# Layer 0's experts by slots and one-expert tiles instead of all experts for all tokens

## Chip, core and metric

The kernel runs on one core of one Trainium2 chip. The metric is the device time of one execution in microseconds. The engines have the profile's names: PE is TensorE (PEld its weight loads), DVE VectorE, ACT ScalarE, POOL GpSimd, SP SyncE; a name with q (SPq, POOLq) is that engine's queue, where DMAs are issued.

## What is computed

Four images of 256 channels and 32 x 32 pixels pass through two layers. Layer 0 is attention in which each row keeps its largest scores, and then a mixture of 8 experts on the 4096 tokens. Layer 1 is a selective scan in four directions, and then a second mixture of 8 experts. Everything is float32. The part that the change concerns is layer 0's mixture:

```python
def _moe(tokens, router_w, w1, b1, w2, b2):      # tokens 4096 x 256, 8 experts
    logits = tokens @ router_w.T
    probs = softmax(logits)
    rw, re = top_k(probs, 2)
    rw = rw / maximum(rw.sum(-1), 1e-12)
    combine = zeros.at[token, re].set(rw)         # two weights per token, six zeros
    out = tokens
    for e in range(8):
        h = gelu(tokens @ w1[e] + b1[e])          # 256 -> 256
        y = h @ w2[e] + b2[e]                     # 256 -> 256
        out = out + combine[:, e:e + 1] * y
    return out

t = t + _moe(_ln_t(t), ...)                       # _ln_t: layer norm over the channels
```

So each token needs two of the eight experts; the other six are multiplied by zero. Layer 1's mixture has the same form, with 1024 hidden channels.

## The kernel before

The program is one long straight line of five stages. The images stay in SBUF as `x[b]`, channels on the partitions (two groups of 128), 1024 tokens along the row. A tile framework allocates buffers from pools (`bufs` is the number of buffers of one name), puts in semaphores, and orders the instructions of each engine by its own priorities, except inside `manual_schedule`, where the written order holds.

**Attention (0 to 1912.6 us)** has a hand-written order. Near its start (`i == 3`, L882) SP issues one DMA that fills `slots_x`, a buffer of 33 MB in DRAM, with zeros from SBUF; layer 1 needs it later. The four residual loads `x_res` (L422) follow on SP's queue over the stage. At the end a value `bad` is loaded into a register of every engine, and a branch (L1066) skips a slow alternative.

**Layer 0's experts (1912.6 to 2522.5 us)** are dense. For each image `layer_norm` writes the normalised tokens `tn[b]`, and matmuls (L1217) give the logits of all images in one PSUM tile. `top2` makes from them `comb`, the two weights of each token and zeros elsewhere. `start_acc` sets the accumulator to the sum of the weighted second biases. Then the loops run over 8 experts, 4 images and 2 halves of 512 tokens:

- L1241: four matmuls `hp` (128 x 128 weights, 512 tokens), as two output groups by two input groups
- L1243: `Gelu` on ACT into `hid`
- L1248: eight matmuls `y`, two for each 128 tokens, now with the tokens on the partitions
- L1250: DVE adds `y` times the token's weight to `acc`

A float32 matmul appears as two records in the profile. Weights of an expert (512 KB) are loaded two experts ahead. In the last expert's loop `acc` is transposed back and added to `x[b]` (L1258, L1260). After image 0, `Prep(0)` prepares the first scan: a layer norm over channels, projections and softplus (`delta`, `dx`).

**Scans (2522.5 to 3782 us)** have a hand-written order as well. DVE's scans set it. While image b + 1 is scanned, `norm(b)` and `route(b)` of layer 1 run step by step in between (each `yield` is one step): `norm` makes the layer norm and the logits of an image, with the tokens as rows of 258 numbers in `tok`; `route` finds the two best experts of each token and gives each (token, choice) pair a *slot*, a row of `slots_x`. Each expert has a region of 16 blocks of 256 slots. `scatter` writes each token's row to its two slots, one indirect DMA on POOL for 128 rows.

**Layer 1's experts (3782 to 4329 us)** then work on tiles of T = 256 slots of one expert. A table, filled by `Tiles.fill`, says for tile i which expert and which block it takes; SP loads the two numbers into registers and issues the DMAs with them as addresses. At most 39 tiles (`NTILE`) are possible; 36 (`USUAL`) always run, and the others behind a branch on `extra`. Tiles whose blocks are full early start before the last image is routed. The results go by indirect DMAs to two rows per token in `results` (L1751).

**The final read (4329 to 4373 us)** loads `results` in eight pieces of 1 MB with four buffers (L1804), weights and adds the two rows of each token (L1808, L1809), transposes them (L1812), adds to `x[b]` (L1815) and writes the output (L1816). Reads and writes are both issued by SP, in turn.

Of the kernel before, what the change touches and what calls it, by code (L numbers as in the profile page):

```python
# [21 lines left out]
P = 128  # L22
# [36 lines left out]
def metaformer(ctx: ExitStack, tc: tile.TileContext, t: dict, out: bass.AP):  # L59
# [70 lines left out]
    def top2(lg, pool):  # L130

        def t3(name):
            return pool.tile([P, NTA, E], F32, tag=name, name=name)

        def t2(name):
            return pool.tile([P, NTA], F32, tag=name, name=name)

        def wide(a):
            return a.unsqueeze(2).to_broadcast([P, NTA, E])

        prob, red = t3("tk_prob"), t2("tk_red")
        nc.vector.tensor_reduce(red, lg, AX.X, ALU.max)
        nc.vector.tensor_tensor(prob, lg, wide(red), ALU.subtract)
        nc.scalar.activation(prob, prob, AF.Exp)
        nc.vector.tensor_reduce(red, prob, AX.X, ALU.add)
        nc.vector.reciprocal(red, red)
        nc.vector.tensor_tensor(prob, prob, wide(red), ALU.mult)

        score, rest, comb = t3("tk_score"), t3("tk_rest"), t3("tk_comb")
        order = first.unsqueeze(1).to_broadcast([P, NTA, E])  # L150

        def best(src, value, onehot):

            nc.vector.tensor_reduce(value, src, AX.X, ALU.max)
            nc.vector.tensor_tensor(score, src, wide(value), ALU.is_equal)
            nc.vector.tensor_tensor(score, score, order, ALU.mult)
            nc.vector.tensor_reduce(red, score, AX.X, ALU.max)
            nc.vector.tensor_tensor(onehot, score, wide(red), ALU.is_equal)

        m1, m2, hot1, hot2 = t2("tk_m1"), t2("tk_m2"), t3("tk_hot1"), t3("tk_hot2")  # L160
        best(prob, m1, hot1)
        nc.vector.scalar_tensor_tensor(rest, hot1, -2.0, prob, ALU.mult, ALU.add)
        best(rest, m2, hot2)
        tot = t2("tk_tot")
        nc.vector.tensor_tensor(tot, m1, m2, ALU.add)
        nc.vector.tensor_scalar(tot, tot, 1e-12, None, ALU.max)
        nc.vector.reciprocal(tot, tot)
        nc.vector.tensor_tensor(comb, hot1, hot2, ALU.add)
        nc.vector.tensor_tensor(comb, comb, prob, ALU.mult)
        nc.vector.tensor_tensor(comb, comb, wide(tot), ALU.mult)  # L170
        return comb


    def start_acc(acc, comb, b2, pool, psum, tag):
        for g in range(NTA // 4):
            ct_ps = psum.tile([E, 4, P], F32, tag=tag, name="ct_ps")
            for i in range(4):
                nc.tensor.transpose(ct_ps[:, i, :], comb[:, g * 4 + i, :], ident)
            ct = pool.tile([E, 4, P], F32, tag="ct", name="ct")
            nc.scalar.copy(ct, ct_ps)  # L180
            for i in range(4):
                y0 = psum.tile([P, C], F32, tag=tag, name="y0")
                nc.tensor.matmul(y0, ct[:, i, :], b2, start=True, stop=True)
                nc.scalar.copy(acc[:, g * 4 + i, :], y0)

    dram = ctx.enter_context(tc.tile_pool(name="slots", bufs=1, space=bass.MemoryType.DRAM))
    slots_x = dram.tile([(E * BLOCKS + 1) * T, W], F32, tag="slots_x", name="slots_x")
    results = dram.tile([2 * B * L + 2 * P, C], F32, tag="results", name="results")  # L190
# [10 lines left out]
    with ExitStack() as st:  # L201
# [644 lines left out]
        with tc.manual_schedule():  # L846
# [33 lines left out]
            for i in range(len(order) + 8):  # L880
                if i == 3:
                    nc.sync.dma_start(slots_x.rearrange("(a p) c -> p a c", p=P),  # L882
                                      zeros.unsqueeze(1).to_broadcast([P, (E * BLOCKS + 1) * T // P, W]))
                turn(i)
# [185 lines left out]
    rt = ctx.enter_context(tc.tile_pool(name="rt", bufs=1))  # L1070
    of_scans = ExitStack()
# [117 lines left out]

    with ExitStack() as st:  # L1190
        wp = st.enter_context(tc.tile_pool(name="m0_w", bufs=1))
        p2 = st.enter_context(tc.tile_pool(name="m0_p2", bufs=2))
        psl = st.enter_context(tc.tile_pool(name="m0_psl", bufs=1, space=PSUM))
        ps2 = st.enter_context(tc.tile_pool(name="m0_ps2", bufs=2, space=PSUM))
        ps3 = st.enter_context(tc.tile_pool(name="m0_ps3", bufs=3, space=PSUM))

        rw = load_rows(wp, "rw0", E)
        b1 = load(wp, "b1_0", [P, E, CT])
        b2 = load(wp, "b2_0", [E, C])

        def weights(e):
            w1 = p2.tile([P, CT, C], F32, tag="w1", name="w1", bufs=3)
            w2 = p2.tile([P, CT, C], F32, tag="w2", name="w2", bufs=3)
            nc.sync.dma_start(w1, t["w1_0"][e].rearrange("(c p) f -> p c f", p=P))
            nc.sync.dma_start(w2, t["w2_0"][e].rearrange("(c p) f -> p c f", p=P))
            return w1, w2

        ahead = [weights(0), weights(1)]

        tn = [wp.tile([P, CT, L], F32, tag=f"tn{b}", name=f"tn{b}") for b in range(B)]  # L1210
        lg = psl.tile([P, NTA, E], F32, tag="lg", name="lg")
        for b in range(B):
            layer_norm(tn[b], x[b], 1e-5, p2, ps2, "m")
            nc.gpsimd.tensor_tensor(x[b], x[b], tn[b], ALU.add)
            for n in range(NT):
                for c in range(CT):
                    nc.tensor.matmul(lg[:, b * NT + n, :], tn[b][:, c, ts(n, P)], rw[:, c, :],  # L1217
                                     start=(c == 0), stop=(c == CT - 1))
        comb = top2(lg, wp)
        acc = wp.tile([P, NTA, C], F32, tag="acc", name="acc")  # L1220
        start_acc(acc, comb, b2, p2, ps2, "m")
        preps = [Prep(0)]

        def room(name, shape):

            if name == "ln_sq":
                return tn[0]
            return p2.tile([P, *shape], F32, tag="ln_sq" if name == "xm" else name, name=name,
                           bufs=1 if name == "sp" else None)

        for e in range(E):
            w1, w2 = ahead.pop(0)
            if e + 2 < E:
                ahead.append(weights(e + 2))
            for b in range(B):
                for h in range(NHALF):
                    hid = p2.tile([P, CT, HALF], F32, tag="hid", name="hid", bufs=3)
                    for f in range(CT):
                        hp = ps3.tile([P, HALF], F32, tag="hp", name="hp")
                        for c in range(CT):  # L1240
                            nc.tensor.matmul(hp, w1[:, c, ts(f, P)], tn[b][:, c, ts(h, HALF)],  # L1241
                                             start=(c == 0), stop=(c == CT - 1))
                        nc.scalar.activation(hid[:, f, :], hp, AF.Gelu, bias=b1[:, e, f : f + 1])  # L1243
                    for i in range(4):
                        n = b * NT + h * 4 + i
                        y = ps2.tile([P, C], F32, tag="y", name="y")
                        for f in range(CT):
                            nc.tensor.matmul(y, hid[:, f, ts(i, P)], w2[:, f, :],  # L1248
                                             start=(f == 0), stop=(f == CT - 1))
                        nc.vector.scalar_tensor_tensor(acc[:, n, :], y, comb[:, n, e : e + 1], acc[:, n, :],  # L1250
                                                       ALU.mult, ALU.add)
                if e < E - 1:
                    continue
                for c in range(CT):
                    for h in range(NHALF):
                        tp = ps2.tile([P, 4, P], F32, tag="m", name="tp")
                        for i in range(4):
                            nc.tensor.transpose(tp[:, i, :], acc[:, b * NT + h * 4 + i, ts(c, P)], ident)  # L1258
                        xs = x[b][:, c, ts(h, HALF)]
                        nc.vector.tensor_tensor(xs, tp.rearrange("p a b -> p (a b)"), xs, ALU.add)  # L1260
                if b == 0:
                    for _ in preps[0].steps(room, ps2, "m"):
                        pass

    rw1 = load(cons, "rw1", [P, CT, E], t["wr1"].rearrange("(c p) o -> p c o", p=P))
    brs = load(cons, "brs", [P, E], t["br1"][0].partition_broadcast(P))

    def kept(name, shape, dt=F32):
        return rt.tile([P, *shape], dt, tag=name, name=name)

    tok = kept("tok", [NT, W])
# [616 lines left out]
```

## Time and profile before

Three runs took 4373.1 us in the median (4371.8 to 4384.0); the profiled execution spans 4373.0 us. Its busy times by stage, from the table of stretches:

| stage | us | PE busy | DVE busy | ACT busy | POOL busy | PE clock | GB/s |
|---|---|---|---|---|---|---|---|
| attention | 1912.6 | 1511.7 | 1592.1 | 1650.7 | 885.1 | 0.79 | 24 |
| layer 0's experts | 609.9 | 588.5 | 185.7 | 168.0 | 18.9 | 0.93 | 8 |
| scans | 1259.5 | 1213.3 | 1152.8 | 914.0 | 624.0 | 0.99 | 112 |
| layer 1's experts | 547.0 | 532.1 | 80.8 | 152.0 | 84.4 | 1.00 | 187 |
| final read | 44.0 | 15.5 | 23.4 | 13.6 | 0 | 0.50 | 286 |

A row is read as a stage with its own limit: an engine that is busy for nearly all of it can set its length, and one that is busy for little cannot. Matmuls are pipelined, so the busy time of a group over its count is the time that one takes from TensorE, while the mean in nanoseconds is its latency. The clock is the share of full speed that was granted to TensorE.

### The profile page before, as it was taken

The page shows a single profiled execution, that of the slowest core. Times are in us where ns is not written, and L with a number is a line of the kernel's source. Part 1 is how long each engine was busy: PE and PEld are TensorE (multiplying, and loading weights), DVE is VectorE, ACT ScalarE, POOL GpSimd, SP SyncE. Part 2 cuts the span into 40 slices and gives each one's busy share as a digit, 9 for nine tenths or more (in the row PEclk, how much of TensorE's full clock was granted, in tenths as well). Part 3 has the DMA queues.
Part 4 walks back from the last instruction along what each step waited for, and adds up shares of the span by engine and source line. Part 5 has one row for each costly group of instructions (what it writes and reads, how often), then busy time and mean ns, then how long its engine had stood idle before and what let it go on. Part 6 is the DMA issues. An engine that isn't in the chain of part 4 may idle for free. (4 is left out here: it accounts for less than half of the span.)

```text
span 4373.0 us, 51176 instructions
## 1 busy us (share of the span) xinstructions
PE 3861.1 (88%) x18522; PEld 2148.5 (49%) x18522; DVE 3034.8 (69%) x5121; ACT 2898.3 (66%) x3800; POOL 1612.4 (37%) x1257
## 2 busy tenths in 40 slices
PE   8378878888888788688999989999999999999996
PEld 5143434343434344345666534444444443588885
DVE  2788898889988988922222489989989989611112
ACT  2989998999999989722111567776877776432222
POOL 0246454644554455520000034444544545321110
PEclk9578877887788778886999999999999999999997
DMA  9200000000000000000000033333423333555555
GB/s 290 72 1 1 11 1 1 1 10 1 1 1 11 1 1 1 11 19 1 10 10 5 2 103 105 119 103 113 128 97 115 121 112 116 178 185 184 192 188 185
DMA packets 171769, 306.80 MB, mean 70 GB/s; under 512 B 27753, under 2 KB 116594, under 8 KB 171506
## 3 DMA queue, kind: packets, MB, share of 16 engines
q1 hardware_dynamic: 161184, 284.10, 20.9%
q0 software_dynamic: 6528, 17.90, 1.1%
q8 instruction: 149, 2.44, 0.2%
q10 hardware_dynamic: 3794, 1.42, 0.1%
q14 instruction: 114, 0.93, 0.1%
HBM read 246.68 MB, written 56.69 MB: 69 GB/s over the span
## 5 line engine op out<-in xcount | busy, mean ns | idle before, releaser
L542 POOL TENSOR_SCALAR dr<-s_n,last 128x1024 bf16<-128x1024 f32 x256 | 731.1, 2873 | 865.1 <-DVE state L570 398.4
L458 ACT ACTIVATE junk_a<-s_n,state 128x1024 int8<-128x1024 f32 x448 | 514.7, 1149 | 27.6 <-DVE state L570 8.0
L1552 POOL TENSOR_TENSOR uu<-dx,bb 128x1024 f32<-128x1024 f32 x128 | 302.4, 2363 | 528.4 <-ACT a_log L1499 528.4
L1585 POOL TENSOR_TENSOR da_c<-prod,come 128x1024 f32<-128x1024 f32 x128 | 244.3, 1909 | 487.6 <-DVE h L1591 433.1
L462 DVE TENSOR_SCALAR_CACHE_REDUCE junk_v<-s_n,state 128x1024 int8<-128x1024 f32 x320 | 408.7, 1277 | 8.8
L1740 ACT ACTIVATE hid<-hp,b 128x256 f32<-128x256 f32 x288 | 133.5, 473 | 355.9 <-PE hp L1738 355.3
L509 DVE SCALAR_TENSOR_TENSOR w<-s_n,win 128x1024 f32<-128x1024 f32 x256 | 352.1, 1375 | 5.3
L1250 DVE SCALAR_TENSOR_TENSOR acc<-y,tk_comb,acc 128x256 f32<-128x256 f32 x256 | 121.0, 484 | 335.9 <-PE y L1248 332.0
L512 DVE MAX8 win<-w 128x8 f32<-128x1024 f32 x256 | 314.5, 1228 | 8.8
L610 ACT ACTIVATE ex<-sT 128x1024 f32<-128x1024 f32 x256 | 246.9, 1015 | 91.5 <-PE sT L602 91.5
L458 ACT ACTIVATE junk_a<-s_n,guess 128x1024 int8<-128x1024 f32 x256 | 294.2, 1149 | 7.4
L1243 ACT ACTIVATE hid<-hp,b 128x512 f32<-128x512 f32 x128 | 87.7, 687 | 318.8 <-PE hp L1241 318.4
L1565 DVE TENSOR_TENSOR_SCAN h<-da,uu 128x1024 f32<-128x1024 f32 x128 | 290.6, 2271 | 4.2 <-DMA cb<-bc_d 4.2
L1591 DVE TENSOR_TENSOR_SCAN h<-da_c,uu 128x1024 f32<-128x1024 f32 x128 | 291.0, 2274 | 0.0
L1574 DVE TENSOR_TENSOR_SCAN h<-da,uu 128x1024 f32<-128x1024 f32 x128 | 289.8, 2264 | 0.0
L620 PE MATMUL o_ps<-ex,vT 128*32 128x256 f32 x2048 | 238.4, 447 | 47.6 <-ACT ex L610 38.1
L1248 PE MATMUL y<-w,hid 128*128 128x256 f32 x1024 | 267.0, 397 | 3.5 <-ACT hid L1243 2.5
L1539 ACT ACTIVATE da_c<-delta,a_log 128x1024 f32<-128x1024 f32 x128 | 268.1, 2095 | 2.5 <-DVE a_log L1500 2.4
L1595 PE MATMUL hp<-h,ident 128*128 128x512 f32 x512 | 248.5, 608 | 22.5 <-DVE h L1591 22.3
L1738 PE MATMUL hp<-xe,w 128*128 128x256 f32 x1152 | 258.6, 381 | 6.4 <-DVE xe L1726 6.2
L492 ACT COPY s_n<-sp 128x1024 f32<-128x1024 f32 x256 | 245.4, 1003 | 24.7 <-PE sp L484 13.2
L1560 PE MATMUL hp<-h,twice 128*128 128x512 f32 x512 | 243.9, 599 | 18.3 <-DVE h L1565 18.2
(519 smaller groups left out, 7946.2 us busy)
## 6 DMA issues: line engine op xcount, KB each, us to landing
bb<-bc_d SPq DMA_DIRECT2D x128, 512.0 KB, 5.0
cb<-bc_d SPq DMA_DIRECT2D x128, 512.0 KB, 4.2
w<-in_w SPq DMA_DIRECT2D x36, 1024.0 KB, 5.3
w2e<-in_w SPq DMA_DIRECT2D x36, 1024.0 KB, 5.6
slots_x<-zeros SPq DMA_DIRECT2D x1, 33282.0 KB
y<-results SPq DMA_DIRECT2D x8, 1024.0 KB, 8.0
xs<-slots_x SPq DMA_DIRECT2D x19, 258.0 KB, 5.4
b2e<-in_b SPq DMA_DIRECT2D x36, 128.0 KB, 5.3
```

What stands on the lines that cost most here:

```text
L458: nc.scalar.activation(junk, self.row(r), AF.Sign, bias=thr, scale=-1.0, accum_out=u)
L462: nc.vector.tensor_scalar(junk, self.row(r), thr, None, ALU.is_lt, ALU.add, accum_out=u)
L509: nc.vector.scalar_tensor_tensor(w, self.row(r), self.win[:, r, 0:1], self.row(r), ALU.is_gt if r < LAST_DVE else ALU.is_ge, ALU.subtract, ...
L512: nc.vector.max(out=self.win[:, r, 1:], in_=w)
L542: ins = nc.gpsimd.tensor_scalar(dr, self.row(r), self.last[:, r : r + 1], None, ALU.is_lt)
L1248: nc.tensor.matmul(y, hid[:, f, ts(i, P)], w2[:, f, :], start=(f == 0), stop=(f == CT - 1))
L1539: nc.scalar.activation(grid(self.da_c), cols_flipped(self.prep.delta[:, self.c]), AF.Exp, scale=self.decay)
L1552: nc.gpsimd.tensor_tensor(self.uu[:, 0], self.prep.dx[:, self.c], self.bb, ALU.mult)
L1565: nc.vector.tensor_tensor_scan(rows.rearrange("p r w -> p (r w)"), self.da, self.uu[:, 0], 0.0, ALU.mult, ALU.add)
L1574: nc.vector.tensor_tensor_scan(hs[:, ::-1], self.da[:, ::-1], self.uu[:, 0][:, ::-1], 0.0, ALU.mult, ALU.add)
L1591: nc.vector.tensor_tensor_scan(hs, self.da_c, self.uu[:, 1], 0.0, ALU.mult, ALU.add)
L1738: nc.tensor.matmul(hp[:, f % 2], self.w1[:, c, ts(f, P)], self.xe[:, c], start=(c == 0), stop=(c == CT - 1))
```

## The change

Layer 0 is given layer 1's method. The definitions of `norm`, `route` and `Tiles` move ahead of layer 0 and get a parameter for the layer; `top2` and `start_acc` go. For each image the tokens are normalised and routed, and a critical section on POOL scatters its rows into `slots_x0` by 16 indirect DMAs and waits for their landing. After the fourth image a table `every` of 39 entries is filled, and the tiles run: SP loads block and expert into registers, reads 256 slots and the expert's weights, and writes the tile's result to the same block of `slots_y0`. The biases of all experts stay in SBUF; DVE, which loads the expert's number as well, copies the two that a tile needs. At the end 64 indirect reads fetch each token's two results, and DVE weights and adds them. Both DRAM buffers are filled with zeros during attention, so that unused slots hold numbers. Separately, the final read gets eight buffers and issues all its loads at once, and the output DMAs move to POOL's queue.

```diff
             for i in range(len(order) + 8):
+                if i in (20, 36):
+                    nc.sync.dma_start((slots_x0 if i == 20 else slots_y0).rearrange("(a p) c -> p a c", p=P),
+                                      zeros[:, :C].unsqueeze(1).to_broadcast([P, (E * BLOCKS + 1) * T // P, C]))
...
-        for b in range(B):
-            layer_norm(tn[b], x[b], 1e-5, p2, ps2, "m")
-            nc.gpsimd.tensor_tensor(x[b], x[b], tn[b], ALU.add)
-            for n in range(NT):
...
-        comb = top2(lg, wp)
-        acc = wp.tile([P, NTA, C], F32, tag="acc", name="acc")
-        start_acc(acc, comb, b2, p2, ps2, "m")
...
+        for b in range(B):
+            d = pb.tile([P, CT, L], F32, tag="d", name="d")
+            here = slot0[:, :, ts(b, NT)]
+            for _ in norm(b, 0, tokens[b], pb, ps_n, "t", "t", d):
+                pass
+            for _ in route(b, 0, None, here, wp.tile([P, 1536], F32, tag="numbers", name="numbers"), ps_n, "t"):
+                pass
+
+            with tc.tile_critical(name=f"scatter{b}", no_gpsimd_drain=True):
+                for n in range(NT):
+                    for k in range(2):
+                        nc.gpsimd.indirect_dma_start(
+                            out=slots_x0, out_offset=bass.IndirectOffsetOnAxis(ap=here[:, k, n : n + 1], axis=0),
+                            in_=tokens[b][:, n], in_offset=None).then_inc(scattered, 16)
+                nc.gpsimd.wait_ge(scattered, 16 * 2 * NT * (b + 1))
...
+        def tile0(i):
...
+            block = register(1, E * BLOCKS, [mybir.EngineType.SP])
+            xs = pb.tile([P, T // P, C], F32, tag="xs", name="xs", bufs=4)
+            nc.sync.dma_start(xs, blocks_x[bass.ds(block, 1)].rearrange("o p a c -> p (o a) c"))
+            e = register(0, E - 1, [mybir.EngineType.SP, mybir.EngineType.DVE])
+            w1 = pb.tile([P, CT, C], F32, tag="w1", name="w1", bufs=3)
...
+            b2e = pb.tile([P, C], F32, tag="b2e", name="b2e")
+            nc.vector.tensor_copy(b2e, b2[:, bass.ds(e, 1)].rearrange("p o d -> p (o d)"))
+            tp = ps1.tile([P, CT, T], F32, tag="tp", name="tp")
...
+            nc.vector.tensor_copy(xe, tp)
...
+                    nc.tensor.matmul(hp[:, f], w1[:, c, ts(f, P)], xe[:, c], start=(c == 0), stop=(c == CT - 1))
+                nc.scalar.activation(hid[:, f], hp[:, f], AF.Gelu, bias=b1e[:, f : f + 1])
...
+                    nc.tensor.matmul(yp[:, a], hid[:, f, ts(a, P)], w2[:, f, :], start=(f == 0), stop=(f == CT - 1))
+            ys = pb.tile([P, T // P, C], F32, tag="ys", name="ys", bufs=4)
+            nc.vector.tensor_tensor(ys, yp, b2e.unsqueeze(1).to_broadcast([P, T // P, C]), ALU.add)
+            nc.sync.dma_start(blocks_y[bass.ds(block, 1)].rearrange("o p a c -> p (o a) c"), ys)
+
+        for i in range(USUAL):
+            tile0(i)
...
+        with tc.If(more_tiles > 0):
+            for i in range(USUAL, NTILE):
+                tile0(i)
...
+                    for k in range(2):
+                        y.append(pb.tile([P, C], F32, tag=f"y{k}", name="yk", bufs=4))
+                        nc.gpsimd.indirect_dma_start(
+                            out=y[k], out_offset=None, in_=slots_y0,
+                            in_offset=bass.IndirectOffsetOnAxis(ap=slot0[:, k, n : n + 1], axis=0))
+                    own = tokens[b][:, h * 4 + i]
+                    nc.vector.scalar_tensor_tensor(y[0], y[0], wts[:, 0, n : n + 1], own, ALU.mult, ALU.add)
+                    nc.vector.scalar_tensor_tensor(y[1], y[1], wts[:, 1, n : n + 1], y[0], ALU.mult, ALU.add)
...
-            pc = sc.enter_context(tc.tile_pool(name="m1_c", bufs=4))
+            pc = sc.enter_context(tc.tile_pool(name="m1_c", bufs=B * NHALF))
...
+            for g in range(B * NHALF):
+                ys.append(pc.tile([P, 4, 2 * C], F32, tag="y", name="y"))
+                nc.sync.dma_start(ys[g], pairs[g])
...
-                        nc.sync.dma_start(out[b].rearrange("(c p) n -> p c n", p=P)[:, c, ts(h, HALF)], xs)
+                        nc.gpsimd.dma_start(out[b].rearrange("(c p) n -> p c n", p=P)[:, c, ts(h, HALF)], xs)
```

## The prediction

> **What bounds the kernel now.** I cut the span into stages with the table of stretches, the borders being the first and last instruction of each stage in the order of time.
>
> ```profile
> core 0: us, PE busy (x) PEld busy (x) DVE busy (x) ACT busy (x) POOL busy (x), PEclk, DMA share, GB/s
> ...
> 1912.60:2522.50 609.90, 588.50 (x2128) 377.50 (x2128) 185.74 (x396) 168.00 (x245) 18.89 (x10) 0.93 0.03 8
> ...
> 3782.00:4329.00 547.00, 532.07 (x2517) 454.42 (x2515) 80.80 (x225) 151.95 (x326) 84.38 (x88) 1.00 0.58 187
> 4329.00:4373.00 44.00, 15.54 (x64) 10.97 (x64) 23.36 (x48) 13.64 (x32) 0.00 (x0) 0.50 0.82 286
> ```
>
> The first row is layer 0's experts, all that the change rebuilds: 609.9 us, in which TensorE is busy 588.5 (96%) and the DMA engines 3%. The second is layer 1's experts, which already work by slots and tiles; it is my price list. The third is the final read. The groups of the first row:
>
> ```profile
> L1248 PE MATMUL y<-w,hid 128*128 128x256 f32 x1024 | 267.0, 397 | 3.5 <-ACT hid L1243 2.5 <-DVE acc L1250 0.9
> L1241 PE MATMUL hp<-tn,w 128*128 128x512 f32 x512 | 244.6, 598 | 0.0
> L1243 ACT ACTIVATE hid<-hp,b 128x512 f32<-128x512 f32 x128 | 87.7, 687 | 318.8 <-PE hp L1241 318.4 <-PE y L1248 0.3
> ```
>
> Two lines are 511.6 us of matmul with almost no idle time; ScalarE and VectorE wait for TensorE. So arithmetic bounds this stage, and it runs all 8 experts for all 4096 tokens where two are used. The same work in layer 1, by tiles of 256 tokens:
>
> ```profile
> L1746 PE MATMUL yp<-w2e,hid 128*128 128x256 f32 x1152 | 255.9, 379 | 0.0
> L1751 POOL DMA_INDIRECT results<-ys,to x72 | 69.0, 959 | 408.9 <-DVE ys L1749 193.1 <-DMA results<-ys,to 167.9 <-DMA xa<-slots_x 29.9
> L1749 DVE TENSOR_TENSOR ys<-yp,b2e 128x512 f32<-128x512 f32 x36 | 24.9, 691 | 320.0 <-PE yp L1746 320.0
> L1723 PE MATMUL tp<-ident,xs 128*128 128x128 f32 x76 | 9.9, 273 | 0.0
> ```
>
> Busy time over count: a 256-wide matmul record takes 0.222 us of TensorE (379 ns is its latency), a transpose 0.130. An indirect DMA holds GpSimd 0.96 us. Its spacing and landing, and a register load with a branch, from the order of time and the issues:
>
> ```profile
> 3863.11 0.96 POOL L1751 DMA_INDIRECT results<-ys,to  x1 [5.21 <-DMA results<-ys,to]
> 3864.37 0.96 POOL L1426 DMA_INDIRECT slots_x<-tok,slot  x1 [0.31 <-issue]
> ...
> 1907.47 0.14 DVE L1063 TENSOR_SCALAR bad<-tot 1x1 int32<-1x1 f32 x1 [0.56 <-PE tot L1062]
> 1912.59 0.37 SPq L1204 DMA_DIRECT2D w<-in_w  x1
> ...
> results<-ys,to POOLq DMA_INDIRECT x72, 5.3
> slots_x<-tok,slot POOLq DMA_INDIRECT x64, 4.7
> ```
>
> Back to back they start 1.26 us apart and land in 4.7 to 5.3 us; the branch costs 5.0 us from the last result to the first instruction behind it.
>
> **What the Trainium skill says.** "TensorE: Matmul & The Clock Gate", Part 1: TensorE runs at half clock unless busy, and falls back after some 3.4 us idle. The trace agrees: granted clock 0.78 in the stage's front (1912.6 to 2009, norms and routing) and 1.00 in the dense layer 1 loop; so a tile loop that idles little keeps its clock. "DMA: Bandwidth & Descriptors", "Latency and other measured facts": a register load takes at least some 0.6 us. On SyncE here a load and the next issue fit into 0.54 us (4105.94 to 4106.48), so I take 0.5. Same page, "Issuing engines are not separate DMA queues": the starting engine saves only issue time, all share 16 engines. The trace fits: the final read runs at 0.82 share with SyncE issuing alternately, so the outputs' move to GpSimd is worth little by itself. "Runtime: NRT & Kernel Launch", "Instruction fetch mechanics": a taken branch can stall for the fetch of its target; the 5.0 us above would hold that, the register and the barrier.
>
> **The change, part by part.** It takes away the whole 609.9 us and puts six pieces in its place.
>
> 1. *Norm and routing, four images one after another.* In the changed program's instruction order VectorE begins an image only after the last slot of the one before, as the logits, the scratch and the counts are single. One image, by rows of the trace: mean matmuls and first subtraction 3.6 (1912.65 to 1916.28) and 1.3; first transposes 0.7; ScalarE four times a copy 0.59 and two squares with their read 0.56 each, 6.9; root 0.4; five small VectorE operations at 0.2 and the scaling and subtraction, 1.7; eight scalings on ScalarE at 0.50, which stand ahead of the exponential, 4.0; table load 1.28 and exponential 0.3; 16 operations of 0.22 to the two hot vectors, 3.5; sums 0.8; the rest, 3.3; hops between engines, 0.7. Sum 28.5; the later three hide their mean behind the slots, 25. Together 103.5 us.
> 2. *Scatter.* Sixteen indirect DMAs per image, 16 x 1.26 + 4.7 = 24.9 us on GpSimd, beside the next image's 25; nobody but the tiles waits for it. Only the last shows: 24.9.
> 3. *First tile:* register 0.5, slots landing 5.4 (row of xs<-slots_x), transposes and copy 1.5: 7.4.
> 4. *36 tiles.* Counting the two best of every token on the reference's own inputs gives 935, 1040, 985, 958, 1123, 1163, 1090 and 898 slots per expert, 4 or 5 tiles each, 36 in sum: just the unconditional ones. TensorE per tile: 16 records x 0.222 + 4 x 0.130 = 4.07. Beside it VectorE: copy and bias sum 0.69 each, two copies of biases and a register load about 1.0; 2.4. ScalarE 2 x 0.47. SyncE: two register loads, four issues with addresses at 0.6, 3.4. DMA: 1.05 MB at 187/0.58 = 322 GB/s, 3.3. All are under 4.07. On SyncE a weight load waits for the matmuls that free its buffer, and the write of a result for VectorE; the loads queued behind are for tiles three or four ahead, with some 7.5 us until due against 5.4 to land. The copy of a tile's transposes comes on VectorE behind the previous bias sum, so I add 0.3 of TensorE waiting: 4.4 x 36 = 158.
> 5. *Drain and branch:* sum 0.7, write landing 5.3, register and branch 5.0: 11.
> 6. *Gathering.* 64 indirect reads. None is in this trace; lower bound the scatter's 0.96 each (61), upper a wait for buffers: eight in flight, each held for the longest landing of these DMAs, 10.3, and some 3.8 of issue and work, 1.76 each (113). I take 1.26: 80.6, then landing 5.3 and the last weighting, transposes and sum 2.8: 88.7. The preparation of the first scan starts after 16 of them (28 us) and took 68 us (2449 to 2517) with table switches between its functions and the experts', some 55 without; 83, beside the gathers. As VectorE and TensorE hold both in one order, each will wait a little for the other: 5 more.
>
> Sum 103.5 + 24.9 + 7.4 + 158 + 11 + 88.7 + 5 = 398.5, against 609.9: **-211 us**.
>
> *Two fills of 33.8 MB with zeros*, issued early in attention behind other loads. The present one, of 33.3 MB, runs from 10.9 to about 131; the counting activation (L458) takes 1.148 us inside and 1.149 later, so nothing on the engines pays. The next residual load comes 410 us later, when the 118 us are over: 0 (up to 5 for a residual load that shares the engines with the fill's start).
>
> *Final read.* Moves 12.6 MB in 44 us, with single slices at 400 GB/s and others near none: a read waits for one of four buffers, and for SyncE's output issues ahead of it. Eight reads at once need 8.4 MB/0.4 = 21 us after the first landing at 5.6; then 5 of work (L1808 to L1815 of one half), 5 for the last output and 2 for output traffic in between: 39. **-5** (0 to -8).
>
> Total 4373.1 - 211 - 5 = **4157 us**.
>
> **Rivals.** *The tiles are fed too late.* Every tile shows a landing and an issue, 5.3 + 0.6 = 5.9 us: 1.5 x 36 = 54 more, 4211. For it: four ordered DMAs per tile on one queue, and only 2 us of slack in the 7.5 of lead. Against: 1.05 MB in 4.4 us is 239 GB/s of 322. *The scatter stops all engines.* It is a critical section that waits for landing; if the next image must wait for it, 3 x 24.9 = 75 more, 4232. Against: in the instruction order no other engine names that wait. *No overlap at all between tiles:* register 0.5, slots 5.4, 1.5, matmuls and Gelu 4.2, sum 0.8, write 5.3 = 17.7 each, 637 instead of 158: 4636, slower. Against: buffers of 2 to 4 and loads three tiles ahead.
>
> **How the numbers follow.** Forecast 0.65, late feeding 0.17, stopped engines 0.13, no overlap or another large cost 0.05. The low end takes 4.07 per tile (-12), gathers near 0.96 (-19), tail -8: 4120; the high end reaches past late feeding alone (4211), since gathers at their upper bound (+32) can meet a forecast otherwise right, and so takes in stopped engines too: 4235. Faster 0.95, same 0.01, slower 0.04.
>
> **What would show it.** Layer 0's experts near 400 us; 36 tiles at 4.1 to 4.6 us with the clock at 1.0 and TensorE over 90% busy; the scatter of images 0 to 2 beside VectorE's work; GpSimd setting the end of the gathering; attention, scans and layer 1 unchanged within a few us. Wrong if a tile takes 6 us or more, if routing takes over 35 us an image, or if attention grows.

## The result, and the profile after

The changed kernel takes 4176.67 us (median of 4 runs, 4162.9 to 4185.63), the kernel before 4372.45 in the same session (4 runs, 4362.23 to 4384.03): a ratio of 0.9549, 95% interval 0.9513 to 0.9584. That is 196 us less; the forecast was 216 less than 4373.1. The profiled execution took 4183.9 us. Its table of stretches, cut at the first and last instruction of each stage, is to be held against the rows of before:

```profile
core 0: us, PE busy (x) PEld busy (x) DVE busy (x) ACT busy (x) POOL busy (x), PEclk, DMA share, GB/s
...
1921.40:2051.00 129.60, 50.41 (x240) 36.35 (x240) 51.48 (x239) 49.55 (x129) 62.61 (x70) 0.61 0.22 78
2051.00:2212.80 161.80, 154.18 (x720) 125.17 (x720) 62.53 (x141) 34.09 (x72) 0.00 (x0) 0.97 0.77 231
2212.80:2331.30 118.50, 48.78 (x144) 26.22 (x144) 60.71 (x123) 29.39 (x37) 63.22 (x64) 0.58 0.26 75
...
4137.70:4183.90 46.20, 15.57 (x64) 10.94 (x64) 23.26 (x48) 13.65 (x32) 8.72 (x16) 0.50 0.73 273
```

The first three rows stand where one row of 609.9 us stood. The one stage in which TensorE was 96% busy is now three: routing and scatter (TensorE 39% busy), tiles (95%), gathering (41%). Together 409.9 us, 200 less. The matmuls shrank most; the two stages around them, in which no engine is busy for more than about half of the time, are 60% of what is left. The last row is the final read: 46.2 us against 44.0, although its reads are now all issued at once.

Two readings carry the rest. In the gathering, GpSimd stops once, for 26.85 us. From the order of time, GpSimd's own instructions (start, duration, engine, line, operation; in brackets the idle time before and what ended it):

```profile
2251.60 0.94 POOL L1476 DMA_INDIRECT yk<-slots_y,slot  x1 [1.22 <-DVE yk L1481]
2252.85 1.11 POOL L1476 DMA_INDIRECT yk<-slots_y,slot  x1 [0.30 <-DVE ln_r L1311]
2280.81 0.94 POOL L1476 DMA_INDIRECT yk<-slots_y,slot  x1 [26.85 <-PE op L1483]
2282.06 0.94 POOL L1476 DMA_INDIRECT yk<-slots_y,slot  x1 [0.30 <-issue]
```

What ended the stop is a token transpose (op, L1483), which frees a y buffer. TensorE in the same stretch:

```profile
2255.00 3.78 PE L1322 MATMUL ln_rb<-ident,ln_rs 128*128 128x128 f32 x16 [4.27 <-DVE ln_rs L1315]
2258.71 3.97 PE L1332 MATMUL bp<-xm,wbc 128*32 128x512 f32 x8
2262.62 7.13 PE L1352 MATMUL zp<-xm,wd 128*128 128x512 f32 x16
2277.61 1.12 PE L1483 MATMUL op<-ident,yk 128*128 128x128 f32 x4 [7.86 <-ACT sp L1362]
```

Between 2240 and 2277 TensorE works only for the first scan's preparation (L1290 to L1352). Then the transposes still wait 7.86 us, for an activation of the preparation, L1362, which reads a zp product out of PSUM: op and the preparation share the three buffers of tag t.

### The profile page after: what moved, and what is told of

It reads as the page before. It is cut to its first block, busy times and chain, and to the rows that moved or that the text cites. A ratio compares the mean times of both kernels' runs of the same rounds, so it can differ in the third digit from the quotient of the medians.

```text
span 4183.9 us, 50091 instructions
## 1 busy us (share of the span) xinstructions
PE 3535.3 (84%) x17498; PEld 1962.6 (47%) x17498; DVE 3020.8 (72%) x5228; ACT 2843.0 (68%) x3792; POOL 1727.9 (41%) x1397
## 5 line engine op out<-in xcount | busy, mean ns | idle before, releaser
L1566 POOL TENSOR_TENSOR uu<-dx,bb 128x1024 f32<-128x1024 f32 x128 | 302.4, 2363 | 7.2 <-DMA bb<-bc_d 7.2
L1761 PE MATMUL yp<-w2e,hid 128*128 128x256 f32 x1152 | 255.9, 379 | 0.0
L1764 DVE TENSOR_TENSOR ys<-yp,b2e 128x512 f32<-128x512 f32 x36 | 24.9, 691 | 316.7 <-PE yp L1761 316.7
L1567 ACT COPY uu<-uu 128x1024 f32<-128x1024 f32 x128 | 253.3, 1979 | 0.2 <-POOL uu L1566 0.2
```

Source lines behind the costliest of these rows:

```text
L1566: nc.gpsimd.tensor_tensor(self.uu[:, 0], self.prep.dx[:, self.c], self.bb, ALU.mult)
L1761: nc.tensor.matmul(yp[:, a], self.hid[:, f, ts(a, P)], self.w2[:, f, :], start=(f == 0), stop=(f == NF - 1))
```

## The experiments

Executions of one and the same program differ by 16 to 38 us (the kernel before, in one session, 4352.27 to 4390.54), and attention, the same code in all but for the fills, ended anywhere between 1893.9 and 1919.1 us in the profiled ones. The intervals of all the ratios from e1 to e6 overlap that of the changed kernel. So I read each experiment in its own stage, of which there is one profiled execution per kernel, and give the whole time beside it.

### What stops the gathers: banks (e1)

```diff
-                for _ in preps[0].steps(room, ps_n, "t"):
+                for _ in preps[0].steps(room, Banks(), "t"):
...
+        class Banks:   # a ring: (ps_h, "hp"), (ps_h, "hp"), (ps1, "tp"), (ps1, "yp")
```

> The first scan's preparation takes its PSUM tiles in a ring of four banks that only the expert tiles used (hp twice, tp, yp) and no longer from the three of tag t, which the token transposes (op) of the gathering need. Theory A (the 26.85 us stop of the gathers comes from the three shared PSUM banks, held by zp until ScalarE has read them): the gathers of the second image resume when TensorE is through the last zp product, at the latest some 17 us after they stopped instead of 28, and the stretch from the last tile's result to the first scan falls from 118.5 to about 108. Theory B (TensorE's order alone makes the stop, the transposes stand behind the zp products): nearly the same, within 3 us of 118.5. Theory C (the preparation's own chain of 62 us sets the end, not the gathers): 118.5 stays. Whole kernel 4166 under A, 4176 under B and C.

Whole: 4150.76 us, ratio 0.9502 (0.9461 to 0.9542). From the first gather to GpSimd's first product of the scans (uu, L1566 of the changed kernel, where it takes 118.5 us) it takes 95.4 us (2206.43 to 2301.87). The longest pause of GpSimd and TensorE's order in e1:

```profile
2260.75 1.01 POOL L1485 DMA_INDIRECT yk<-slots_y,slot  x1 [2.79 <-PE op L1492]
```

```profile
2236.44 1.09 PE L1492 MATMUL op<-ident,yk 128*128 128x128 f32 x4
2237.32 3.41 PE L1303 MATMUL ln_var<-mean_w,ln_sq 128*128 128x1 f32 x16
2240.60 1.48 PE L1492 MATMUL op<-ident,yk 128*128 128x128 f32 x4
2243.80 0.66 PE L1492 MATMUL op<-ident,yk 128*128 128x128 f32 x2 [1.72 <-DVE ln_rr L1312]
```

The shared banks are the cause, theory A, but the gain is 23 us where A expected 10. The lines show why: with banks of its own the preparation no longer orders itself against the transposes, and the scheduler places transposes between its steps, ahead of the zp products. I had let that order stand. So the shared buffers acted twice, by the wait of 7.86 us and by the order that they forced; how the 23 us divide between the two, no run shows.

### Order instead of banks, and deeper buffers (e2, e3)

```diff
# e2: as e1, and
-                for _ in preps[0].steps(...): pass
+                coming = preps[0].steps(room, Banks(), "t")
...
+                    if b > 0:      # behind the transposes of each token group
+                        next(coming, None); next(coming, None)
# e3: the changed kernel, and
-   y.append(pb.tile([P, C], F32, tag=f"y{k}", name="yk", bufs=4))
+   y.append(pb.tile([P, C], F32, tag=f"y{k}", name="yk", bufs=9))
```

> As the kernel with own banks, and the preparation's steps are written two at a time between the token groups of images 1 to 3, so that the transposes of a group no longer stand behind all of the preparation on TensorE. Theory A or B (waiting of the gathers for y buffers, through TensorE's order or its banks): no gap over 3 us between gathers, 64 x 1.25 + 3 to land + 3 of work = 86 after the first gather, about 92 from the last tile's result to the first scan instead of 118.5; whole kernel about 4150. Theory C (the preparation's chain sets the end): its steps now wait for groups that come every 2.5 us, so it ends as late or later, 118.5 or more; whole kernel 4176 or more.

> Nine buffers per y tag instead of four, nothing else. Theory A or B: GpSimd runs five pairs further before it stops, 10 x 1.25 = 12.5 us of the stop are used, and the stretch falls from 118.5 to about 106; the stop itself is then some 14 us. Theory C: 118.5.

e2: 4155.16 us, ratio 0.9522 (0.9476 to 0.9569); e3: 4165.6 us, ratio 0.9537 (0.9494 to 0.958). GpSimd's order of time, first e2, the last gather and the first scan product, then e3, the gather that ends its stop:

```profile
2279.97 0.94 POOL L1485 DMA_INDIRECT yk<-slots_y,slot  x1 [0.30 <-issue]
2295.63 2.44 POOL L1580 TENSOR_TENSOR uu<-dx,bb 128x1024 f32<-128x1024 f32 x1 [14.71 <-DMA bb<-bc_d]
```

```profile
2278.68 0.94 POOL L1476 DMA_INDIRECT yk<-slots_y,slot  x1 [18.83 <-PE op L1483]
```

In e2 all gathers run without a stop, 82.4 us from first to last (2197.59 to 2279.97), but the stretch is 98.0, not 92: the preparation, written between the groups, now holds up the end. Its last delta product (dx, L1342) stands on VectorE at 2290.65, between the last two token sums (2290.04 and 2291.25), which waited behind its steps. The scan's first load (bb) is issued at 2291.47, 11.5 us after the last gather's start, where e1 takes 4.2 (2293.60 to 2297.80). So theories A and C are both partly right: with the stop gone, the preparation costs some 7 us. e3 takes 108.0 us (2205.80 to 2313.79): 10.5 less, near the 12.5 expected; its stop is 18.83, where some 14 were expected. Deeper buffers bridge part of a stop, banks remove it.

### The exponential ahead of the token scalings (e4)

```diff
-   for n in range(NT):                      # in norm, layer 0
-       nc.scalar.mul(tok[:, n, :C], tok[:, n, :C], s1[:, n : n + 1])
+   yield s1
...
+   next(todo)                               # route up to behind its exponential
+   for n in range(NT):
+       nc.scalar.mul(tokens[b][:, n], tokens[b][:, n], s1[:, n : n + 1])
```

> Layer 0's eight token scalings on ScalarE are written behind the router's exponential, so that the exponential no longer stands behind them. Theory (the exponential's place in ScalarE's order holds VectorE, 4.16 us of wait per image): an image takes 21 to 22.6 us instead of 25, then GpSimd's scatter of 16 x 1.26 + 2.4 = 22.6 sets the distance; norm, routing and scatter fall from 129.6 to 118 to 122, whole kernel 4166. Rival (the scatter, or the scalings that it needs, bound the stage already): 129.6 stays within 2 us.

4167.53 us, ratio 0.9551 (0.9509 to 0.9593). VectorE's order of time, first the changed kernel, the sum behind the exponential of image 0, then e4, the slots of image 1:

```profile
1941.53 0.22 DVE L1111 TENSOR_REDUCE numbers<-lg 128x8 f32<-128x64 f32 x1 [4.16 <-ACT lg L1110]
```

```profile
1949.88 0.17 DVE L1167 CAST slot<-numbers 128x8 int32<-128x8 f32 x1 [2.33 <-POOLq L1406]
```

The first wait fell to 1.77 us, as meant; in its place VectorE waits 2.33 for GpSimd to finish the scatter of the image before, since all images' slots lie in one tile (e9, with a tile per image, no longer has this wait). From the first mean to the first tile it is 126.4 us (1899.82 to 2026.22) against 129.8: -3.4, so mostly the rival. The images stay 24.7 us apart. That number adds up: scatter start to the end of VectorE's wait 22.2, its last slot operations 0.8, to the next start 1.7.

### The final read (e5, e6)

```diff
# e5
-   nc.gpsimd.dma_start(out[b].rearrange(...)[:, c, ts(h, HALF)], xs)
+   nc.sync.dma_start(out[b].rearrange(...)[:, c, ts(h, HALF)], xs)
# e6: e5, and reads as before
-   pc = sc.enter_context(tc.tile_pool(name="m1_c", bufs=B * NHALF))   # all reads ahead of the loop
+   pc = sc.enter_context(tc.tile_pool(name="m1_c", bufs=4))           # each read in the loop
```

> The final read's sixteen outputs are issued by SyncE again, the eight reads stay at once at the head. Theory A (outputs sent from GpSimd land about 10 us after their issue, those of SyncE 3.5): the final read takes about 40 instead of 46.2 us. Theory B (the reads at once fill the DMA engines, and the outputs wait behind them whoever sends them): 45 to 47. Whole kernel 4170 under A, 4176 under B.

> The final read as in the kernel before: four buffers, each read issued when its turn comes, outputs on SyncE; all of layer 0 as in the changed kernel. The forecast's step (reading at once saves 5 us): the final read takes 51. The trace of the changed kernel (46.2 against 44.0 before) says 44. Under the theory that reading at once is good and only GpSimd's outputs are bad it is also above the run with outputs on SyncE by 3 to 5.

e5: 4172.44 us, ratio 0.9548 (0.9502 to 0.9593), final read 38.2 us (4137.2 to 4175.4). e6: 4167.16 us, ratio 0.954 (0.9494 to 0.9586), final read 44.4 (4137.5 to 4181.9). VectorE's last sum and the span, first of the changed kernel, then of e5:

```profile
core 0 of [0], span 4183.9 us
...
4171.85 1.29 DVE L1834 TENSOR_TENSOR x<-op,x 128x512 f32<-128x512 f32 x2 [0.67 <-PE op L1831]
```

```profile
core 0 of [0], span 4175.4 us
...
4170.76 1.29 DVE L1834 TENSOR_TENSOR x<-op,x 128x512 f32<-128x512 f32 x2 [0.68 <-PE op L1831]
```

The engines finish at almost the same distance from the stage's start, 35.4 and 34.9 us; after the last sum it takes 10.8 us to the end with GpSimd sending, 3.3 with SyncE. The time is theory A's, but its mechanism is not: the outputs land much alike (median 5.5 us from GpSimd, 5.0 from SyncE), and the changed kernel's last two 2.4 us after their issue. What the DMA engines moved from 4137 to 4184 in the changed kernel, in 40 slices of 1.2 us:

```profile
GB/s 0 91 279 357 345 345 387 406 396 384 387 368 303 415 406 413 404 399 408 410 401 422 404 408 404 420 389 87 279 167 0 220 227 0 0 0 0 0 0 0
```

After 4176 nothing moves and no engine is busy for the last 7.9 us. In e5 the last bytes have moved by 4173.9, 1.5 us before the end. All six profiled kernels that send the outputs from GpSimd end 10.7 to 10.8 us after the last sum, and the eight that use SyncE 3.3 to 3.6. So the sender is the cause, and it acts behind the last transfer; what fills that time the traces don't show. Reading at once does save: 6.2 us between e6 and e5. The outputs' move to GpSimd took it back, and 2 us more.

### The fills (e7) and the tiles (e8)

```diff
# e7: the kernel before, and in attention's loop
+   if i in (20, 36):
+       nc.sync.dma_start((slots_x0 if i == 20 else slots_y0).rearrange(...), zeros...)
# e8: the changed kernel, and
+   for i in range(USUAL):
+       tile0(i)
```

> The kernel before with only the two zero fills of 33.8 MB added in attention, at the places where the change puts them; the filled tensors are not used. Forecast (the fills cost nothing): attention ends as in the kernel before, within the 10 us by which executions of one program differ, and a ratio of 1.000 within 0.002. Rival (the fills slow the loads or the tables of attention): 5 to 10 us more, beginning at the first fill and growing behind it, ratio 1.001 to 1.0025.

> The 36 expert tiles of layer 0 are run twice, with the same results. Forecast (a tile costs TensorE's 4.07 us and 0.3 of waiting, loads and writes are beside it): 36 x 4.4 = 158 us more, 4335. Late feeding (a tile costs a landing and an issue, 5.9): 212 more, 4389. No overlap (17.7 per tile): 637 more.

e7: 4362.53 us against 4364.2, ratio 0.9994 (0.9976 to 1.0013). The fills cost nothing that can be measured; the interval leaves room for at most some 6 us. Attention had ended 9 us later in the changed kernel's profile; its loads (SyncE's order of time), first the changed kernel, then e7:

```profile
532.43 0.37 SPq L366 DMA_DIRECT2D x_res<-in_x  x1
532.85 0.46 SPq L826 DMA_DIRECT2D slots_x<-zeros  x1
963.55 0.37 SPq L366 DMA_DIRECT2D x_res<-in_x  x1
```

```profile
514.20 0.37 SPq L423 DMA_DIRECT2D x_res<-in_x  x1
514.62 0.46 SPq L883 DMA_DIRECT2D slots_x<-zeros  x1
940.88 0.37 SPq L423 DMA_DIRECT2D x_res<-in_x  x1
```

The difference is already there at the first of these loads, ahead of the first new fill: 532.43 here, 523.29 before, 514.20 in e7. So it isn't the fills; why executions of the same program differ so in attention stays open.

e8: 4324.61 us, ratio 0.9921 (0.9895 to 0.9946). From the first tile to the first gather it takes 319.1 us (2035.48 to 2354.56) against 165.4 (2051.40 to 2216.76): 153.7 for 36 tiles more, 4.27 us each. Late feeding (5.9) and no overlap (17.7) are out. The second pass in the table of stretches:

```profile
2195.00:2350.50 155.50, 149.96 (x719) 122.23 (x717) 62.28 (x141) 34.10 (x72) 0.00 (x0) 1.00 0.78 234
```

At full clock TensorE is busy 96%. The groups of the tiles' stretch in the changed kernel name its waits: a first product for the copy of the transposes (VectorE) and a weight load for the Gelu (ScalarE); none waits for a load, but for the first tile's.

```profile
L1443 PE MATMUL hp<-xe,w 128*128 128x256 f32 x288 | 85.8, 403 | 6.3 <-DVE xe L1438 1.6 <-ACT hid L1444 0.6
L1448 PE MATMUL yp<-w,hid 128*128 128x256 f32 x288 | 74.3, 381 | 0.1
L1436 PE MATMUL tp<-ident,xs 128*128 128x128 f32 x144 | 22.6, 281 | 29.5 <-DMA xs<-slots_x 29.5
```

### Put together (e9 to e12)

```diff
# e9: e1, e4, e5, and a slot tile per image
-   slot0 = wp.tile([P, 2, NTA], I32, tag="slot0", name="slot0")
+   slot0 = [wp.tile([P, 2, NT], I32, tag=f"slot0_{b}", name="slot0") for b in range(B)]
# e10: e9, and
-   nc.gpsimd.wait_ge(scattered, 16 * 2 * NT * (b + 1))
    if b == B - 1:
+       nc.gpsimd.wait_ge(scattered, 16 * 2 * NT * B)
# e11: e10, and nine y buffers as in e3
# e12: e1, e4, e5 alone
```

> The changed kernel with four edits together: the preparation's own banks (e1), the exponential ahead of the token scalings (e4), outputs of the final read on SyncE (e5), and new, one slot tile per image instead of one for all. The run with the exponential first showed VectorE waiting 2.3 us per image to write its slots until GpSimd's scatter of the image before had landed. Theory (that wait is the shared slot tile): the distance between the first scatters of two images falls from 24.7 to about 22.5, the first scatter to the first gather by some 6 us against the changed kernel's 264.9; with -23 of the banks and -8 of the outputs the whole is about 4137. Rival (the scatter must have landed in any case before the next image's may start, so GpSimd sets 24.7): no gain in the routing, about 4143.

> As the combined kernel, and GpSimd waits for the scatter's landing only after the last image (the tiles are the first to read the slots). Theory (GpSimd's wait is part of the cycle): images come at VectorE's own distance, 22 to 22.5 us, and the last scatter starts up to 3 us earlier than in the combined kernel. Rival (VectorE's routing sets the distance): equal to it within 1 us.

> As the kernel with the single wait, with nine y buffers per tag instead of four. If GpSimd's gathers set the end of layer 0 (87.2 us from first to last gather with own banks, 80 unstopped): 5 us less there. If the preparation on ScalarE and VectorE sets it: no change.

> The preparation's own banks, the exponential ahead of the token scalings and the final outputs on SyncE; the slot tile is one for all images again, as in the changed kernel. In the combined kernels the images came 28 to 31.5 us apart instead of 24.7, with VectorE standing 4 to 10 us at small copies of the logits during a scatter. Theory (those stops come with the slot tile per image, which lets VectorE run on without waiting for GpSimd): the distance is 24.7 again, and the gains add up, -23, -5 and -8 against the changed kernel, about 4141. Rival (the three edits together make the stops): 28 to 31.5 us as before, about 4155.

e9: 4158.4 us, ratio 0.9505 (0.9479 to 0.9531). e10: 4151.7, 0.95 (0.9479 to 0.952). e11: 4171.95, 0.9537 (0.9511 to 0.9563). e12: **4141.07**, 0.9488 (0.9461 to 0.9515), the lowest of all, though its interval overlaps those of e1 to e6 and of e9 to e11. e9 failed both of its theories: the images came further apart, not nearer. VectorE's order of time in e9, the small copies of the logits during one scatter:

```profile
2006.14 0.17 DVE L1220 COPY lg<-raw 128x16 f32<-128x16 f32 x1 [1.41 <-PE nm_tp L1216]
2010.83 0.17 DVE L1220 COPY lg<-raw 128x16 f32<-128x16 f32 x1 [4.52 <-remote]
2019.38 0.17 DVE L1220 COPY lg<-raw 128x16 f32<-128x16 f32 x1 [8.38 <-remote]
```

The product that the last copy reads had ended at 2013.7, so it stood ready for 5.7 us. "Remote" is the profile's word for a releaser that it can't place. First scatters came 28.0, 29.6 and 31.5 us apart. e10 has the same stops, up to 9.8 us, and starts its last scatter no earlier, 88.8 us after the first (e9: 89.1); the gathers begin 276.8 us after the first scatter in both. e11 has them too, in the gathering as well (one of 21.0 us on VectorE), so its question on deeper buffers can't be read. e12 differs from e9 by the slot tiles alone, and GpSimd's starts of its four scatters are at the old distance:

```profile
1927.43 1.25 POOL L1409 DMA_INDIRECT slots_x<-tok,slot  x1 [26.86 <-DVE d L1207]
1952.11 0.95 POOL L1409 DMA_INDIRECT slots_x<-tok,slot  x1 [4.46 <-DVE d L1207]
1976.81 0.96 POOL L1409 DMA_INDIRECT slots_x<-tok,slot  x1 [4.75 <-DVE d L1207]
2001.35 0.95 POOL L1409 DMA_INDIRECT slots_x<-tok,slot  x1 [4.56 <-DVE every_expert L1064]
```

So the stops go with the tile per image: the three kernels that have it show them, the nine with one tile for all do not, and e12 differs from e9 in nothing else. As each was profiled once, and e9 to e11 in one session and e12 in another, this points to the tile but is not proof. How it would make the stops is open. The Trainium skill, "SBUF — State Buffer", section "SBUF: two separate sides", says that GpSimd and VectorE share one pair of ports under an exclusive lock, which a VectorE operation needs in a two-port mode or with two inputs in SBUF. The copies that stood have one input, in PSUM, and e12 has the same copies beside the same issues without a stop, so the lock alone doesn't explain it.

e12's gains add up in its own stages: routing and scatter 126.5 (-3.1), tiles 160.8 (-1.0), first gather to first scan product 95.5 (-23.0), final read 38.3 (-7.9): 35 us, and the medians differ by 35.6. By ratios it is 27; the intervals of the two touch (0.9515 and 0.9513), so the sum of stages is the better witness.

## Why the prediction was right, and where it was off

The sign, the mechanism and the size held: 399 us forecast for layer 0, 410 measured; a whole of 4157 against 4176.67, inside the range. By its own steps:

1. *Norm and routing* (forecast 103.5): from the start of the stage to the last scatter's start 105.4. Right. It called the distance of 25 us VectorE's alone; e4 showed that GpSimd's cycle of 24.7 us through the shared slot tile stands just under it, so that a faster VectorE gains little. The rival of stopped engines was thus partly there, hidden.
2. *Last scatter and first tile* (24.9 + 7.4): last scatter's start to the first tile's transposes 24.6. The landings were too dear: 4.7 taken, 2.4 measured for a scatter, 5.4 taken, 2.7 for the tile's slots. They had come from stages with other traffic.
3. *Tiles* (158): 161.4, the first one's start included; e8's added tile costs 4.27 where 4.4 was said. Right.
4. *Drain and branch* (11): last sum to first gather 4.0. The write landed in 3.5, not 5.3, and as 4.0 for all of it is less than the 5.0 given to the branch alone, the branch ran beside the landing and was cheaper; I had added them.
5. *Gathering* (88.7 and 5 for the coupling): 114.5 to the scan's first load. The spacing was right, 1.25 us where 1.26 was taken, and a gather lands in 2.8. The step that failed is the coupling term: "each will wait a little for the other: 5 more" was a stop of 26.85 us. I had named one order on VectorE and TensorE, but hadn't looked at which PSUM tag the preparation takes. e1 shows that the tag is the cause.
6. *Final read* (-5): +2.2. Half of the step was right, reading at once saves 6.2 us (e6 to e5). What failed is that the outputs' move "is worth little by itself": it costs 8 us, 7.9 us of the changed kernel being an end in which nothing moves. I had read the Trainium skill's "DMA: Bandwidth & Descriptors", section "Issuing engines are not separate DMA queues" (all engines' transfers run on the same 16, the starter saves only issue time), as if the starter made no other difference. e5 measures one of 8 us. The same page, "Issuing engine by pattern", puts simple loads and stores on SyncE, and the runs agree.
7. *Fills* (0): nothing measurable, by e7. Attention's 9 us came ahead of them, so the prediction's sign of being wrong, "if attention grows", was met by the spread of executions and not by the fills.

In layer 0 the steps' errors sum to +1.9 - 7.7 + 3.4 - 7.0 + 20.8 = +11.4 us: landings and a branch that had been taken too dear paid for 15 of the 21 us that the coupling term missed. That the sum came so near is in this part luck. Scans and layer 1 stayed, 1260.7 and 545.7 us against 1259.5 and 547.0.

## What to carry to other kernels

When an arithmetic-bound stage is cut to what is needed, the work around it becomes the stage: here routing and gathering are 60% of it. A buffer tag shared in the gathering cost 23 us, while the estimate of all 36 tiles was off by 3.4. Before two chains of work are said to lie beside each other, look at every pool tag they share, in PSUM too, since a shared tag sets their order as well as their waits. Leave plain outputs that end a kernel on SyncE, which was worth 8 us here, and try each edit of a combination alone: with the fourth edit in e9, about half of what the other three won was lost again.

## What the hardware showed unexpectedly

- A kernel that ends on plain outputs sent by GpSimd ended 10.8 us after its last sum, against 3.3 when SyncE sent them, although the last bytes had moved by 4176.0 of 4183.9 us.
- Scatters and gathers of 128 rows of 1 KB started 1.25 to 1.26 us apart and landed in 2.4 and 2.8 us in stages with little other traffic (78 and 75 GB/s, mostly their own), where an indirect write took 5.3 in layer 1 (187 GB/s). That the traffic makes the difference is not tested.
- With one slot tile per image, VectorE stood 3 to 10 us at operations of 0.17 us during scatters, and 7.5 to 21 us once during the gathers; with one tile for all there was no such stop. The cause is open.
- The attention stage, the same in all kernels but for the fills, ended between 1893.9 and 1919.1 us. Why is open.
